# Moving the operands of a feed-forward block to other SBUF addresses: two pads, a pool for the statistics, two small buffers fewer

## The chip, the cores and the metric

The kernel runs on one core of a Trainium2 chip. The metric is the device time of one execution in microseconds; the number to compare is the median of several runs. Five engines take part: TensorE (PE in the profile; PEld is its loading of weights), VectorE (DVE), ScalarE (ACT), GpSimd (POOL) and SyncE (SP), which issues most of the DMAs. SBUF is the on-chip memory that PE, DVE, ACT, POOL and the DMAs share; a tile in it occupies the same byte range in each of 128 partitions, so that one number, its start within the partition, gives its address.

## What is computed

One transformer block over x of shape (4, 1024, 256), in float32: attention with 16 heads, then a gated feed-forward part with ternary weights and two square hidden layers of 1024 x 1024. Cut to what matters:

```python
x = x + layernorm(attention(layernorm(x), Wqkv, Wout))
# feed-forward part, on y = layernorm(x); tlin(x, w, s) = einsum('bsi,oi->bso', x, w) * s
h = silu(tlin(y, w1_w, w1_s)) * tlin(y, w2_w, w2_s)      # 256 -> 1024
h = gelu(tlin(h, h1_w, h1_s))                            # 1024 -> 1024
h = gelu(tlin(h, h2_w, h2_s))                            # 1024 -> 1024
x = x + layernorm(tlin(h, w3_w, w3_s))                   # 1024 -> 256
```

## The kernel before

Everything is unrolled; the order of instructions on each engine is the order in which the Python code issues them, and semaphores are placed where one engine's result is another's input. `tile_fast` does the whole block. `tile_general` is a fallback that runs only when a flag computed on the chip is set; in the traced execution it isn't.

**Attention** takes the four batches in turn, to about 575 us. For each batch and group of four heads, line 536 makes the scores `s` from the stacked tiles `sq` and `sk`, line 537 exponentiates them into a ring of eight half-tiles `e`, and line 544 weighs the values, `acc <- e, vaug`. Preparing the next batch (line 321 projects `xT` with `wqk_sb` and `wv_sb`), rounding the feed-forward weights and dividing by the sums (`quotients`, with its small tile `den`) are put between as side steps.

**The feed-forward part** then takes each batch of 1,024 tokens as two halves of 512. Its matmuls run on float32r values: each float32 operand is split into a rounded part `hi` (line 936, ScalarE) and a remainder `lo` (line 940, VectorE), and both are multiplied with the same ternary weights, which are exact.

- `gated`: line 966 multiplies `x_in` (four tiles that were `cq`/`ck` in the attention) with `w1` and `w2` (also in former `cq`/`ck` tiles) into the PSUM tile `pg`; ScalarE's silu and one VectorE instruction follow. Per batch 128 matmuls of 128x128 weights against 128x512 columns.
- `Layer.run`, twice: the square layers are done with a scheme of seven block products in place of eight. The weights' seven factors were made during the attention, lie in DRAM, and come by DMA (`load_factor`) into a ring of four slots, which are the former `sq`/`sk` tiles (`ring_of`). Line 1045 multiplies them with the `hi` and `lo` of sums of hidden blocks, into the PSUM tile `ph`. Per batch 448 matmuls of the same form as those of `pg`. The weights are the stationary operand and are loaded for each matmul; the `hi` or `lo` block is the moving operand, whose columns are streamed.
- `finish`: line 1153 multiplies the last hidden blocks (here the stationary operand) with `w3_sb` (the moving one, 256 columns) into `pz`, 128 matmuls per batch; layer norm, residual and store follow.

The hidden blocks (`Half`: `g`, `hi`, `lo`, `t2`, `c`, `u`, `w`, each [128, 2, 512] of 4 bytes, 4,096 bytes per partition) come from a free list of 22 places. Eight, `a0` to `a7`, are opened on the left side of SBUF where the ring `e` was, fourteen, `b0` to `b13`, by `open_ffn` in the pool `fb` on the right side, where the attention's pools `aw` and `work` were. Pools are laid one behind another, from the left upwards and from the right downwards, and each tile takes the next multiple of 32 bytes. So the small tiles ahead of a large one decide its address modulo 256:

| tiles | start modulo 256, before | after |
|---|---|---|
| `cq`/`ck` (in `gated`: x_in, w1, w2), `sq`/`sk` (ring of factors), ring `e`, `a0` to `a7` | 128 | 0 |
| `w3_sb` | 32 | 0 |
| `b` blocks | 160 (one), 32 (three), 224 (ten) | 0 |
| `xT`, `xn`, `top`, `wr`, `vaug`, `on`, `wqk_sb`, `wv_sb`, `wo_sb`, `cv`, `folded`, `oT` | 160 | 0 |
| `x0` to `x3` (inputs and residuals) | 224 | 224 |

Each operand's start within such a tile is a multiple of 512 bytes further on in lines 966, 1045 and 1153, so it has the tile's remainder.

`Norms` holds the small statistics of the layer norms (`mv`, `st`, `ve`, `rstd`, `nb`); its attribute `small` says which pool they come from. In the feed-forward part that is `fb`, where they lie between the `b` blocks, six buffers each.

Of the kernel before, what the change touches and what calls it, by code (L numbers as in the profile page):

```python
# [10 lines left out]
F32 = mybir.dt.float32  # L11
# [8 lines left out]
P = 128  # L20
HEADS = 16
DH = 16
SLOT = 32
# [14 lines left out]
NQ = 512  # L38
# [5 lines left out]
@with_exitstack  # L44
def tile_attention_ffn_block(ctx: ExitStack, tc: tile.TileContext, x, wqk, wv, wo, w1, w1s, w2, w2s, h1, h1s, h2, h2s, w3, w3s, out):

    nc = tc.nc
    B, S, D = x.shape
    bad = ctx.enter_context(tc.tile_pool(name="flag", bufs=1)).tile([1, 1], I32, name="bad")
    tile_fast(tc, x, wqk, wv, wo, w1, w1s, w2, w2s, h1, h1s, h2, h2s, w3, w3s, out, bad)
    failed = nc.values_load(bad[0:1, 0:1], min_val=0, max_val=1 << 24)
    with tc.If(failed > 0):  # L70
        tile_general(tc, x, wqk, wv, wo, w1, w1s, w2, w2s, h1, h1s, h2, h2s, w3, w3s, out)
# [58 lines left out]
def tile_fast(ctx: ExitStack, tc: tile.TileContext, x, wqk, wv, wo, w1, w1s, w2, w2s, h1, h1s, h2, h2s, w3, w3s, out, bad):  # L130
# [12 lines left out]
    small = ctx.enter_context(tc.tile_pool(name="small", bufs=3))  # L143
# [28 lines left out]
    norms = Norms(nc, const, small)  # L172
# [23 lines left out]
    with ExitStack() as actx, ExitStack() as rctx:  # L196
        aw = actx.enter_context(tc.tile_pool(name="aw", bufs=1, side="right"))
# [50 lines left out]
        on = [aw.tile([P, DC, NQ // SLOT, SLOT], F32, name=f"on{h}") for h in range(NH)]  # L248

        heads_bf = aw.tile([P, SLOT], BF16, name="heads_bf")  # L250
        nc.vector.memset(heads_bf, 0.0)
        own = small.tile([P, HPT], F32, tag="own", name="own", bufs=1)
        nc.vector.tensor_reduce(own, ident.rearrange("p (h d) -> p h d", d=DH), AX.X, ALU.add)
# [304 lines left out]
        def quotients(g, h, em, o):  # L558

            o = o.rearrange("p (j s) -> p j s", s=SLOT)  # L560
            den = small.tile([P, NQ // SLOT], F32, tag="den", name="den")
            n = P // SLOT
            nc.vector.scalar_tensor_tensor(den[:, 0:n], em, SM_EPS, o[:, 0:n, DH], ALU.mult, ALU.add)
            nc.vector.tensor_copy(den[:, n:], o[:, n:, DH])
            nc.vector.reciprocal(den, den)
            e = DH * (g % GPT)
            nc.vector.tensor_mul(on[h][:, g // GPT, :, e : e + DH], o[:, :, 0:DH], den.unsqueeze(2).to_broadcast([P, NQ // SLOT, DH]))
# [3 lines left out]
        def divide(g, h, o, top):  # L571


            there = shuffle.tile([HPG, P, P], F32, tag="top", name="top_d")
            folded = work.tile([P, P // SLOT, P], F32, tag="folded", name="folded", bufs=1)
            nc.sync.dma_start(out=there.rearrange("i k q -> k i q"), in_=top.rearrange("p u n q -> p (u n) q"))

            mine = divided["made"]
            divided["made"] += 1

            def back():
                nc.sync.dma_start(out=folded, in_=there.rearrange("i (k s) q -> (i k) s q", s=P // SLOT))

            def fold():
                for n in (2, 1):
                    nc.vector.tensor_max(folded[:, 0:n], folded[:, 0:n], folded[:, n : 2 * n])
                nc.vector.transpose(folded[:, 1], folded[:, 0])

            def run():
                em = small.tile([P, P // SLOT], F32, tag="em", name="em")  # L590
                nc.vector.tensor_reduce(em, folded[:, 1].rearrange("p (j k) -> p j k", k=SLOT), AX.X, ALU.max)
                quotients(g, h, em, o)
                divided["done"] += 1

            begun = Step(back, 2, False)
            begun.ready = lambda: divided["done"] == mine
            return [begun, Step(fold, 2, False, work=1.2), Step(run, 1, False, work=1.4)]

        def divide_last(g, h, o, top):


            def run():
                turned = work.tile([P, P // SLOT, P], F32, tag="folded", name="turned", bufs=1)
                flat, n = top.rearrange("p u n q -> p (u n q)"), HPG * P // SLOT
                nc.vector.transpose(turned.rearrange("p s q -> p (s q)"), flat)
                nc.vector.tensor_reduce(flat[:, 0:n], turned.rearrange("p s (j k) -> p (s j) k", k=SLOT), AX.X, ALU.max)
                parts = flat[0:SLOT, n : n + n * P // SLOT].rearrange("p (k n) -> p k n", n=n)
                for k in range(P // SLOT):
                    nc.vector.tensor_copy(parts[:, k], flat[SLOT * k : SLOT * (k + 1), 0:n])
                most = flat[0:SLOT, P : P + n]  # L610
                nc.vector.tensor_reduce(most, parts.rearrange("p k n -> p n k"), AX.X, ALU.max)
                most = most.rearrange("p (i j) -> p i j", i=HPG)
                em = small.tile([P, P // SLOT], F32, tag="em", name="em")
                for i in range(HPG):
                    nc.vector.tensor_copy(em[SLOT * i : SLOT * (i + 1), :], most[:, i])
                quotients(g, h, em, o)

            return [Step(run, 1, False)]

        def ending(b, h, copy):  # L620
# [61 lines left out]
            if b < B - 1:  # L682

                return steps + [Step(lambda: side.add(tail), 0, False)]
            opened = Step(open_ffn, 0, False)
            opened.ready = lambda: not ends[b, 0][0]
            return steps + ([opened] if h == NH - 1 else []) + tail
# [65 lines left out]
        side = Side()  # L753
# [94 lines left out]
        def load_weights(n, chunks=None):  # L848
            for c in range(len(homes[n])) if chunks is None else chunks:
                nc.sync.dma_start(out=homes[n][c].bitcast(F32), in_=rounded[n][c * P : (c + 1) * P, :].bitcast(F32))  # L850
# [10 lines left out]
        def open_ffn():  # L861

            actx.close()
            fb = ctx.enter_context(tc.tile_pool(name="fb", bufs=1, side="right", reuse_waits="tile"))
            free.extend((fb, f"b{i}") for i in range(14))
            w3_sb = fb.tile([P, HC, D], F32R, name="w3_sb")
            homes["w3"] = [w3_sb[:, c, :] for c in range(HC)]
            load_weights("w3")
            ffn["fb"] = fb
            norms.small, norms.bufs = fb, 6  # L870

        def norm_steps(tiles, st):

# [794 lines left out]
```

## Time and profile before

| what | value |
|---|---|
| median of 3 runs (lowest, highest) | 1205.7 us (1205.09, 1208.14) |
| the profiled execution: its own time, its span | 1206.14 us, 1204.4 us |
| mean granted TensorE clock | 0.994 |
| busy: PE, PEld, DVE, ACT, POOL | 1160.6, 709.1, 845.9, 886.2, 298.7 us |
| DMA moved | 163.66 MB, mean 136 GB/s |
| chain that ended last, largest parts | PE 71%; by line: PE ph L1045 35%, PE acc L544 10%, PE pg L966 9% |

The span is the time from the first to the last instruction of the profiled execution; its own time adds what lies around it. The duration given for a matmul includes the time until its result has drained: a matmul of `ph` has a duration of 394 ns in the middle, while the next one starts long before that. What a matmul costs when they follow each other closely is therefore the distance from its start to the next one's, which the timeline's first column and the chain of waits give. In the chain, a row is a run of instructions of one group, with its start, its length and its count.

### The profile page before, as it was taken

What the parts mean: (1) busy time and instruction counts of PE and PEld (TensorE: products, weight loads), DVE (VectorE), ACT (ScalarE), POOL (GpSimd) and SP (SyncE); (2) the same over time, 40 slices, a digit from 0 to 9 for tenths busy, and PEclk for the clock granted to TensorE, in tenths of its full rate; (3) what the DMA queues carried; (4) which work ended last, traced back from release to release, by engine and by line L of the source; (5) the groups of instructions that cost most, each with busy time, mean ns of one, the idle gap of its engine ahead of it and who ended that gap; (6) DMA issues with size and microseconds to landing.
All of it is one profiled execution on the core that took longest, in us unless ns stands there. A gap on an engine that the chain in (4) does not pass through costs nothing.

```text
span 1204.4 us, 21320 instructions
## 1 busy us (share of the span) xinstructions
PE 1160.6 (96%) x7994; PEld 709.1 (59%) x7994; DVE 845.9 (70%) x1501; ACT 886.2 (74%) x1050; POOL 298.7 (25%) x458
## 2 busy tenths in 40 slices
PE   8999999999999999998999999999999999999994
PEld 3333333333333333332678889888898888988884
DVE  4577777785878867767585756867678676785765
ACT  4999888988999989998466575576756767567660
POOL 6454256565566643220000000000000000000000
PEclk9999999999999999999999999999999999999997
DMA  5877655676666664472314441354522545225401
GB/s 144 214 185 185 150 134 157 163 178 163 155 175 164 167 166 105 106 176 88 105 36 140 134 147 57 101 175 153 179 74 85 177 154 176 74 84 187 157 24 38
DMA packets 78672, 163.66 MB, mean 136 GB/s; under 512 B 14688, under 2 KB 40928, under 8 KB 78560
## 3 DMA queue, kind: packets, MB, share of 16 engines
q1 hardware_dynamic: 62832, 120.18, 34.9%
q0 software_dynamic: 15200, 41.50, 12.6%
q8 instruction: 65, 1.06, 0.4%
q10 hardware_dynamic: 528, 0.52, 0.1%
q14 instruction: 47, 0.39, 0.1%
HBM read 98.71 MB, written 29.88 MB: 107 GB/s over the span
## 4 chain that ended last, share of the span: by engine, by line
PE 71%; DVE 10%; ACT 9%; issue 4%; DMA 3%; SPq 2%; POOL 1%; ACTq 0%; POOLq 0%; DVEq 0%
PE ph L1045 35%; PE acc L544 10%; PE pg L966 9%; ACT e L537 8%; PE s L536 7%; PE pz L1153 4%; PE p L321 2%; DVE top L556 2%; PE py L321 2%; SPq L482 1%; PE pv L321 1%; DVE st L97 1%; DMA x<-in_x_dram 1%; DMA sq<-cq0hi 1%; PE fpt L909 1%
## 5 line engine op out<-in xcount | busy, mean ns | idle before, releaser
L537 ACT ACTIVATE e<-s 128x1024 f32<-128x1024 f32 x512 | 483.0, 1046 | 43.8 <-PE s L536 34.1
L544 PE MATMUL acc<-e,vaug 128*32 128x512 f32 (+1 forms) x2424 | 256.6, 535 | 1.4 <-DVE o L798 1.4
L107 POOL TENSOR_TENSOR rstd<-ve,minus_half 128x4 f32<-128x4 f32 (+1 forms) x34 | 38.3, 1126 | 700.6 <-DVE ve L105 596.2
L536 PE MATMUL s<-sq,sk 64*128 64x512 f32 x1024 | 188.9, 445 | 20.7 <-ACT e L537 19.5
L536 PEld LDWEIGHTS s<-sq,sk 64*128 64x128 f32 x1024 | 87.3, 184 | 167.9 <-ACT e L537 147.4
L1045 PE MATMUL ph<-hi,sq 128*128 128x512 f32 x448 | 177.8, 397 | 0.0
L1045 PE MATMUL ph<-lo,sq 128*128 128x512 f32 x448 | 176.7, 394 | 0.0
L1045 PE MATMUL ph<-hi,sk 128*128 128x512 f32 x448 | 176.6, 394 | 0.0
L1045 PE MATMUL ph<-lo,sk 128*128 128x512 f32 x448 | 176.5, 394 | 0.0
L556 DVE TENSOR_TENSOR top<-top,e 128x512 f32<-128x512 f32 x192 | 140.1, 730 | 21.1 <-ACT e L537 15.4
L544 PEld LDWEIGHTS acc<-e,vaug 128*32 128x32 f32 x2424 | 61.9, 109 | 117.4 <-issue 107.4
L940 DVE TENSOR_TENSOR lo<-g,hi 128x1024 fp32r<-128x1024 f32 x48 | 58.8, 1224 | 57.8 <-ACT hi L936 57.8
L1045 PEld LDWEIGHTS ph<-lo,sk 128*128 128x128 f32 x448 | 84.1, 188 | 20.0
L1045 PEld LDWEIGHTS ph<-hi,sk 128*128 128x128 f32 x448 | 84.1, 188 | 20.0
L1045 PEld LDWEIGHTS ph<-hi,sq 128*128 128x128 f32 x448 | 84.1, 188 | 19.5
L1045 PEld LDWEIGHTS ph<-lo,sq 128*128 128x128 f32 x448 | 84.2, 188 | 19.2
L1033 ACT ACTIVATE c<-ph,h_scale 128x512 f32<-128x512 f32 x64 | 40.5, 684 | 55.8 <-PE ph L1045 55.8
L940 DVE TENSOR_TENSOR lo<-c,hi 128x1024 fp32r<-128x1024 f32 x48 | 58.2, 1219 | 25.8 <-ACT hi L936 25.8
L968 ACT ACTIVATE sg<-pg,w_scale 128x512 f32<-128x512 f32 x64 | 43.9, 687 | 41.6 <-PE pg L966 38.2
L321 PE MATMUL p<-xT,wqk_sb 128*32 128x512 f32 x512 | 65.7, 593 | 0.5 <-ACT xT L324 0.5
L969 DVE SCALAR_TENSOR_TENSOR g<-pg,w_scale,sg 128x512 f32<-128x512 f32 x64 | 47.7, 747 | 22.1 <-ACT sg L968 22.1
L1153 PE MATMUL pz<-w_sb,hi 128*128 128x256 f32 x256 | 60.1, 279 | 0.0
(189 smaller groups left out, 1830.0 us busy)
## 6 DMA issues: line engine op xcount, KB each, us to landing
sq<-h_f SPq DMA_DIRECT2D x56, 512.0 KB, 3.9
sk<-h_f SPq DMA_DIRECT2D x56, 512.0 KB, 4.7
w<-in_h_dram POOLq DMA_DIRECT2D x32, 256.0 KB, 4.9
h_f<-wr POOLq DMA_DIRECT2D x16, 512.0 KB, 3.7
x<-in_h_dram SPq DMA_DIRECT2D x16, 512.0 KB, 3.6
top_d<-top SPq DMA_DIRECT2D x30, 256.0 KB, 2.5
folded<-top_d SPq DMA_DIRECT2D x30, 256.0 KB, 3.6
h_f<-wr POOLq DMA_DIRECT2D x16, 384.0 KB, 3.8
```

The lines of the kernel that those rows point to most:

```text
L321: nc.tensor.matmul(o[j : j + SLOT, :], w[:, j : j + SLOT], i, **flags)
L536: nc.tensor.matmul(s[:, a, :], stacks[1, g % 2, u][r, c * P : (c + 1) * P], stacks[0, g % 2, u][r, h * NQ : (h + 1) * NQ], start=True, sto ...
L537: nc.scalar.activation(pair(k)[:, u], s, AF.Exp)
L544: nc.tensor.matmul(acc[SLOT * i : SLOT * (i + 1), q0:q1], vaug[g % 2][:, c, i, :], pair(k)[:, i // 2, i % 2, q0:q1], start=c == 0 and q0 = ...
L556: nc.vector.tensor_max(top, top if c > 1 else pair(k - 2)[:, :, :, 0:P], pair(k)[:, :, :, 0:P])
L940: nc.vector.tensor_sub(self.lo[i].t, self.raw[i].t, self.hi[i].t.bitcast(F32))
L966: nc.tensor.matmul(p[:, k, :], homes[n][d][:, m * P : (m + 1) * P], half[:, d, :], start=d == j == 0, stop=d == DC - 1 and j == 1)
L968: nc.scalar.activation(sg, p[:, 0, :], AF.Silu, scale=scales["w1"][:, m : m + 1])
L969: nc.vector.scalar_tensor_tensor(x[i, h][c // 2].t[:, c % 2, :], p[:, 1, :], scales["w2"][:, m : m + 1], sg, ALU.mult, ALU.mult)
L1033: nc.scalar.activation(o.t[:, j, :], (o.t if src is None else src)[:, j, :], AF.Gelu, scale=scale[:, m : m + 1])
L1045: nc.tensor.matmul(p[:, j, :], w, half, start=start and c == n == 0, stop=c == HC // 2 - 1 and n == 1, skip_group_check=True,)
L1153: nc.tensor.matmul(p[:, j, :D], half[:, (t0 + j) * P : (t0 + j + 1) * P], homes["w3"][c], start=c == order[0] and n == 0, stop=c == order[ ...
```

## The change

It adds a tile of 160 bytes per partition at the end of the pool `aw` and one of 32 bytes at the beginning of a new pool `fs`; neither is used. `fs` is opened by `open_ffn` ahead of `fb` and takes the statistics of the feed-forward part, which no longer lie between the `b` blocks. `den` has one buffer in place of three (64 bytes each), so that everything behind it on the left side starts 128 bytes earlier. The starts that result are in the table above.

```diff
@@ -248,6 +248,7 @@
         heads_bf = aw.tile([P, SLOT], BF16, name="heads_bf")
+        aw.tile([P, 40], F32, name="even")
         nc.vector.memset(heads_bf, 0.0)
@@ -558,7 +559,7 @@
-            den = small.tile([P, NQ // SLOT], F32, tag="den", name="den")
+            den = small.tile([P, NQ // SLOT], F32, tag="den", name="den", bufs=1)
@@ -861,13 +862,15 @@
             actx.close()
+            fs = ctx.enter_context(tc.tile_pool(name="fs", bufs=1, side="right", reuse_waits="tile"))
+            fs.tile([P, 8], F32, name="even")
             fb = ctx.enter_context(tc.tile_pool(name="fb", bufs=1, side="right", reuse_waits="tile"))
             free.extend((fb, f"b{i}") for i in range(14))
             w3_sb = fb.tile([P, HC, D], F32R, name="w3_sb")
             homes["w3"] = [w3_sb[:, c, :] for c in range(HC)]
             load_weights("w3")
             ffn["fb"] = fb
-            norms.small, norms.bufs = fb, 6
+            norms.small, norms.bufs = fs, 6
```

## The prediction

> **What bounds the kernel now.** I read the engine shares first, then the chain that ended last in order of time, then a table of engine busy time by stretch, then TensorE's rows in order of time. TensorE (PE) is busy 1160.6 us of 1204.4, 96%. The first half (to about 575 us) is attention, in which ScalarE's exponentials run almost as full as PE. In the feed-forward half PE stands alone: in the stretch from 585 to 1182 us it is busy 595.27 of 597.00 us, beside 417.10 for VectorE, 374.70 for ScalarE and a DMA share of 0.36. From 617.95 us on the chain is nothing but matmuls:
>
> ```profile
> 724.08 14.85 PE pz L1153 x128
> 738.93 29.06 PE pg L966 x128
> 768.00 33.49 PE ph L1045 x144
> ...
> 806.29 48.32 PE ph L1045 x208
> ...
> 1068.73 89.15 PE ph L1045 x384
> ```
>
> The columns are start, length, engine, output tile, line, count. Dividing length by count gives the time from one matmul's start to the next: pg 29.06/128 = 227.0 ns; ph 33.49/144 = 232.6, 48.32/208 = 232.3, 89.15/384 = 232.2 ns; pz (256 columns, not 512) 14.85/128 = 116.0 ns. pg and ph have the same form, 128x128 weights against 128x512 float32r columns, yet ph is 5 ns dearer. In this half any nanosecond off a matmul comes off the end, so the question is what these 5 ns are.
>
> Here the profile has to be read with the table of addresses above. Line 1045 has 1,792 matmuls in the trace and 1,792 in the program, so the n-th of one is the n-th of the other, and every row gets its operands' addresses. All of pg's operands, weights and columns, lie at 128 mod 256. ph's weights do too, but its columns lie in blocks at 128, 160, 32 or 224. Here is ph with all four of its column blocks at 224, and then with all four at 128:
>
> ```profile
> 700.67 0.39 PE L1045 MATMUL ph<-hi,sq 128*128 128x512 f32 x1
> 700.90 0.39 PE L1045 MATMUL ph<-lo,sq 128*128 128x512 f32 x1
> ...
> 703.94 0.40 PE L1045 MATMUL ph<-hi,sk 128*128 128x512 f32 x1
> 704.17 0.39 PE L1045 MATMUL ph<-lo,sk 128*128 128x512 f32 x1
> ```
>
> ```profile
> 718.48 0.39 PE L1045 MATMUL ph<-hi,sk 128*128 128x512 f32 x1
> 718.71 0.39 PE L1045 MATMUL ph<-lo,sk 128*128 128x512 f32 x1
> ...
> 722.11 0.39 PE L1045 MATMUL ph<-hi,sk 128*128 128x512 f32 x1
> 722.33 0.39 PE L1045 MATMUL ph<-lo,sk 128*128 128x512 f32 x1
> ```
>
> Sixteen matmuls of the first are 15 steps in 3.50 us, 233.3 ns each; eighteen of the second are 17 steps in 3.85 us, 226.5 ns each. Over all of ph (steps of up to 260 ns) the mean by the column block's place is 231.1 ns at 128 (612 steps), 233.2 at 160 (80), 234.5 at 32 (256), 233.7 at 224 (837). All 20 blocks sort this way: the eight at 128 lie between 229.6 and 232.6, the twelve others between 232.6 and 235.3.
>
> The blocks at 128 are not at 226.7 in the mean because a block at another place leaves something behind. A stretch of operands that all lie at 128, entered after one that does not, steps 233, 236, 224, 231, 236, 228, 233, 231 ns (231.5 in the mean) and then falls to 226-227 and stays. The longest such stretch has 33 matmuls: seven longer steps, then 226 or 227 to its end. I counted pairs of successive steps within such stretches: from 226-227 none of 47 left it in ph and 2 of 407 in pg; of the others 4 of 132 in ph and 11 of 64 in pg fell into it. So the cheap rhythm holds while operands lie alike, and ph is mixed all the time.
>
> **The change part by part.**
>
> **Instructions.** Engine by engine, the changed program has the same instructions in the same order with the same waits in everything that the trace shows executed; only waits ahead of the fallback, which doesn't run, are arranged otherwise. Hence the single buffer for `den` costs nothing: its four users are all VectorE instructions, in order, and no wait comes in. The two pads are never read or written. The statistics in `fs` are small tiles used by VectorE, GpSimd and ScalarE, and no wait comes in for them either. What is left is addresses: every operand of ph, pg and pz goes to 0 mod 256.
>
> **ph.** 1,772 steps of up to 260 ns have a mean of 232.3 ns (411.6 us); 20 longer ones wait for data or follow a pause, and I leave them. No row of the trace has an operand at 0 mod 256. The nearest is 128, the only other place that is a multiple of 64, with pg as a whole stage in which all operands lie alike: 227.3 ns (497 steps). I take that: 1,772 x 5.0 ns = **8.8 us**.
>
> **pz.** 511 steps, mean 116.9 ns. Its moving operand w3_sb (at 32) meets weights at 224, 128, 32 and 160. In the first batch, with weights at 224 only, sixteen in a row step 113-114 ns, half of 226.7; with weights at 128 or 32 it is 116 to 121. At 113.5 the gain is 511 x 3.4 ns = **1.7 us**.
>
> **pg.** Already 227.3; I take nothing (226.7 would be 0.3 us).
>
> **Attention.** Its fp32 matmuls (acc, p, pv, py) have a step of 429-430 ns for four of 512 columns whether the columns lie at 128 (e) or 160 (xT): place doesn't show there, nothing taken. The float32r scores s have all operands at 128 already and step 231 or 235-236 ns behind the fp32 ones; 328 steps of that kind at 6 ns could give 2.0 us, but PE waits 19.5 us for the exponentials there, so part is hidden. I take 0, and 2 us either way for the range.
>
> **Other engines.** VectorE's lo takes 1218 to 1227 ns for every mix of places, ScalarE's hi 1043 to 1051, the gelu 684 at all four: nothing to gain, and nothing that PE would then wait for, since 10 us less PE time raises VectorE's share of this stretch from 417/597 to 417/587 only. The factor loads (512 KB, 3.9 to 4.7 us from issue to landing) have four ring slots ahead of products of 7.4 us.
>
> **Sum.** 8.8 + 1.7 = 10.5 us, all on the chain. The profiled execution took 1206.14 us, of which 1204.4 is span and 1.7 lies around it; the median 1205.7 is 0.4 below it. 1205.7 - 10.5 = **1195.2 us**.
>
> **Two rules weighed.** The row: 226.5 ns where all lies at 128, 233.3 where columns lie at 224. The Trainium skill's page "SBUF — State Buffer" says under "Who interferes with whom" that "PE and ACT never wait on anyone", and under "Operand start alignment" it asks only for a multiple of the element size and calls that legality, not speed. By these rules address is nothing and the sum is 0: 1205.7 us. The row contradicts them in this trace, so I go by the row, and keep the rule as a rival. Second, "TensorE: Matmul & The Clock Gate", in "Wait — 56ns, not 53.3ns?", puts a warm matmul's step at columns / 2.4 GHz plus about 2.5 ns, 215.7 ns for 512 columns. The fp32 rows agree if 512 fp32 columns are counted as 1,024 (429-430 ns), the best float32r row doesn't (226.7, which is 215.7 plus 11). If that rest came from 128 not being a multiple of 256, ph would give 1,772 x 16.6 = 29.4 us, pg 497 x 11.6 = 5.8, pz 511 x 7.7 = 3.9, in all 39 us: 1166.6 us, an estimate by that page. Since 226.7 is seen at a steady 544 cycles of 2.4 GHz, 17 for every 16 columns, it looks like the form's own rate rather than a fault of place. It is the lower end, unlikely.
>
> **Rivals.**
> **Half a gain.** Places no longer disturb, but the dearer rhythm is kept alive by other things (the pauses of about 90 ns between products, ScalarE and VectorE in the same memory). Then ph stays at what its stretches of equal places have now, 230.0 ns: 1,772 x 2.3 = 4.1, and pz gives about 0.8: 1200.8 us. For it: stretches at 128 begin with the longer steps. Against: pg has such pauses too and stays at 227.3.
> **No change.** Either the rule holds and order, not place, makes the difference, or 0 mod 256 keeps the dearer rhythm everywhere: 231.5 ns for ph and pg, 118 for pz gives 1.4 - 2.1 - 0.6 = -1.3 us, 1207.0. Against: twenty blocks sorted by place.
> **Slower: weights and columns meet.** Weights and columns are read at the same time (PEld is busy while PE is), and now both start at 0 mod 256 everywhere. If equal places made them collide, as pz's 118 to 121 ns with weights and w3_sb both at 32 may show, steps would go to the worst seen in bulk, 236 and 120.5: 6.6 + 4.3 + 1.8 = 12.7 us more, 1218.4. It decides from a mean step of 231.5 ns over all three on (584.5 us over 2,525 steps of 512 columns), and from 232.9 it is measurably slower. Against: pg has both at 128 and runs cheapest of all.
>
> **How the numbers follow.** Full gain (1193 to 1198): 0.63. Half a gain (1198 to 1203): 0.14. No change: 0.11. Slower: 0.06. A gain beyond 226.7: 0.06. The range 1190 to 1202.5 holds the first, nearly all of the second and the nearer part of the last, eight in ten. A measurement of this kernel tells from no change about 0.3%, 3.6 us: faster 0.82 (full, beyond, most of half), within it 0.12, slower 0.06.
>
> **What would show it.** Right: ph's groups on the chain at 227 to 228 ns by length over count, pz at 113 to 114, pg still 227, all earlier times on the chain up to 575 us within 2 us. Half: ph at 230. Wrong in size: any step near 216, or pg moved. Wrong altogether: ph at 232 with its columns at 0, or gaps in PE where it now ran through (waits on hi or lo).

## The result and the profile after

The changed kernel takes 1199.88 us (median of 6 runs, 1197.99 to 1202.45), the kernel before 1207.06 us (6 runs, 1205.09 to 1210.02): a ratio of 0.9935, 95% interval 0.9923 to 0.9947. The change is faster by about 7.8 us; 10.5 were predicted.

The same stages of the feed-forward part in the chain of waits of the changed kernel (start, length, engine, output, line, count; line 966 is now 969, 1045 is 1048, 1153 is 1156):

```profile
722.61 15.35 PE pz L1156 x128
737.96 29.04 PE pg L969 x128
767.00 32.66 PE ph L1048 x144
...
1063.82 87.04 PE ph L1048 x384
```

Length over count gives what a matmul costs: ph 32.66/144 = 226.8 and 87.04/384 = 226.7 ns, where it was 232.6 and 232.2; pg 226.9, where it was 227.0; pz 15.35/128 = 119.9 ns, where it was 116.0. So the square layers gained what they could, and the last layer lost. In the timeline of the changed kernel the last layer's starts stand 0.12 us apart:

```profile
729.76 0.28 PE L1156 MATMUL pz<-w_sb,lo 128*128 128x256 f32 x1
729.88 0.28 PE L1156 MATMUL pz<-w_sb,hi 128*128 128x256 f32 x1
...
731.08 0.28 PE L1156 MATMUL pz<-w_sb,hi 128*128 128x256 f32 x1
731.20 0.28 PE L1156 MATMUL pz<-w_sb,lo 128*128 128x256 f32 x1
```

Twelve steps in 1.44 us are 120.0 ns each. Over all matmuls, leaving out steps of more than 260 ns (the granted clock is 1.00 from 618 to 1178 us in every run of this document, so it is no cause of what differs here):

| | ph, 1,772 steps | pg, 497 steps | pz, 511 steps |
|---|---|---|---|
| before | 232.29 ns, 411.6 us | 227.34 ns, 113.0 us | 116.95 ns, 59.8 us |
| after | 227.00 ns, 402.2 us | 227.25 ns, 112.9 us | 119.94 ns, 61.3 us |

That is -9.4 us for ph and +1.5 us for pz, -7.9 in sum. The span fell by 7.2 us only (1204.4 to 1197.2), because the attention half of this execution ended 0.6 us later: the first ph of the chain starts at 618.54 us instead of 617.95. From there to the end it is 578.7 instead of 586.4 us, 7.7 less. PE stays the bound. Of its waits in the feed-forward part (the view of waits, PE alone, 585 to 1182 us: who waits for whom, us in total, times, longest) the only row is, as before the change (there with a longest wait of 1.0),

```profile
PE pg L969 <- DVE g L972: 1.7, 2, 0.9
```

The attention half starts the feed-forward part anywhere between 617 and 622 us in the runs below, with the kernel's own scatter. I therefore compare the **feed-forward stretch**, the time from the first ph row of the chain to the span's end. One kernel profiled twice (`w3_32` and the timed version below) had 577.4 and 577.2 us of it.

### The profile page after: what moved, and what is told of

It is laid out like the page before. It is cut to its first block, busy times and chain, and to the rows that moved or that the text cites. A ratio compares the mean times of both kernels' runs of the same rounds, so it can differ in the third digit from the quotient of the medians.

```text
span 1197.2 us, 21320 instructions
## 1 busy us (share of the span) xinstructions
PE 1153.3 (96%) x7994; PEld 710.4 (59%) x7994; DVE 842.7 (70%) x1501; ACT 886.4 (74%) x1050; POOL 297.8 (25%) x458
## 4 chain that ended last, share of the span: by engine, by line
PE 68%; ACT 9%; DVE 7%; DMA 6%; issue 4%; POOL 4%; SPq 1%; ACTq 0%; POOLq 0%; DVEq 0%
PE ph L1048 34%; PE acc L545 9%; PE pg L969 9%; ACT e L538 8%; PE s L537 6%; PE pz L1156 4%; PE p L322 2%; PE py L322 2%; DMA h_f<-wr 1%; DMA w<-in_h_dram 1%; PE pv L322 1%; DVE top L557 1%; DMA x<-in_x_dram 1%; SPq L483 1%; DMA sk<-ck0lo 1%
## 5 line engine op out<-in xcount | busy, mean ns | idle before, releaser
L943 DVE TENSOR_TENSOR lo<-g,hi 128x1024 fp32r<-128x1024 f32 x48 | 58.8, 1224 | 54.6 <-ACT hi L939 54.6
L943 DVE TENSOR_TENSOR lo<-c,hi 128x1024 fp32r<-128x1024 f32 x48 | 58.2, 1219 | 24.2 <-ACT hi L939 24.2
L1156 PE MATMUL pz<-w_sb,lo 128*128 128x256 f32 x256 | 61.6, 283 | 0.0
```

The lines of the kernel that those rows point to most:

```text
L943: nc.vector.tensor_sub(self.lo[i].t, self.raw[i].t, self.hi[i].t.bitcast(F32))
L1156: nc.tensor.matmul(p[:, j, :D], half[:, (t0 + j) * P : (t0 + j + 1) * P], homes["w3"][c], start=c == order[0] and n == 0, stop=c == order[ ...
```

## The experiments

The theory at the start was the prediction's: the cheap rhythm, 226.7 ns, needs columns at multiples of 64. All runs but the last are a single execution each, so what is read from them is the steps. Each diff below is against the changed kernel. The kernel before, run on the same chip beside them, took 1210.2 us (beside `left_only`, `all128`, `all32`, `w3_64`), 1206.4 (beside `c32_w0`, `c128_w0`, `w3_128`, `w3_192`) and 1209.88 (beside `w3_32`, `w3_160`, `w3_224`).

**One part alone (`left_only`).** Only `den` keeps one buffer; the pad in `aw`, the pool `fs` and its pad are gone. The left side moves to 0, the `b` blocks stay at 160, 32 and 224.

```diff
-        aw.tile([P, 40], F32, name="even")
-            fs = ctx.enter_context(tc.tile_pool(name="fs", bufs=1, side="right", reuse_waits="tile"))
-            fs.tile([P, 8], F32, name="even")
-            norms.small, norms.bufs = fs, 6
+            norms.small, norms.bufs = fb, 6
```

> One part alone: one buffer for den, so cq/ck, the ring of factors and the a blocks lie at 0; the b blocks stay at 160, 32 and 224, w3_sb at 32, and no pool fs. Theory (the cheap rhythm needs the columns of successive matmuls to lie at multiples of 64): pg 227.3 ns a step, ph still 232 (mixed), pz 116 to 118; time 1206 to 1208 us. Rival (0 for the weights is what counts): ph near 227, time near 1197.

1208.62 us. Its chain:

```profile
727.02 15.06 PE pz L1153 x128
742.09 29.05 PE pg L966 x128
771.14 33.36 PE ph L1045 x144
...
1071.28 89.05 PE ph L1045 x384
```

ph is at 231.7 and 231.9 ns (mean 231.78), pz at 117.3: nearly as before the change (232.29 and 116.95). Moving the weights and eight of the 22 blocks to 0 does next to nothing while the other fourteen lie elsewhere.

**Another common place (`all128`).** The left side at 128 as before the change, and the right side moved to 128 too. Against the kernel before, this adds only the pool `fs` with its pad.

```diff
-        aw.tile([P, 40], F32, name="even")
-            den = small.tile([P, NQ // SLOT], F32, tag="den", name="den", bufs=1)
+            den = small.tile([P, NQ // SLOT], F32, tag="den", name="den")
-            fs.tile([P, 8], F32, name="even")
+            fs.tile([P, 40], F32, name="even")
```

> All operands of pg, ph and pz at 128 mod 256, the places of the left side as before the change, the b blocks and w3_sb moved to 128. Theory (128 is as good as 0 for 512 columns): ph and pg 227.0, pz 120 as after the change, time 1199 to 1201 us. Rival (256 is needed): ph 230 or more, time 1205.

1199.32 us, ph 226.95, pg 227.35, pz 119.94 ns, stretch 578.7 us, all as in the changed kernel. Two rows of its chain:

```profile
722.89 15.35 PE pz L1155 x128
...
1064.06 87.04 PE ph L1047 x384
```

So the gain is in putting the `b` blocks where the rest is, and multiples of 256 are not what counts.

**A common place that is no multiple of 64 (`all32`).** A pad of 32 bytes ahead of `cq`, and everything on the right at 32.

```diff
+        keep.tile([P, 8], F32, name="shift")
-        aw.tile([P, 40], F32, name="even")
-            fs.tile([P, 8], F32, name="even")
+            fs.tile([P, 64], F32, name="even")
```

> All operands of pg, ph and pz at 32 mod 256, alike but at no multiple of 64. Theory (a multiple of 64 is needed): ph and pg 231 to 234, time 1207 to 1212 us. Rival (it is enough that operands lie alike): ph and pg 227, time 1200.

1201.34 us. The theory fell, the rival stands:

```profile
725.02 15.35 PE pz L1156 x128
740.37 29.04 PE pg L969 x128
769.41 32.66 PE ph L1048 x144
...
1066.18 87.04 PE ph L1048 x384
```

Each of these rows has the changed kernel's length to the hundredth of a microsecond. At 32 mod 256 the matmuls are as cheap as at 0 or 128, provided that all operands are there; the stretch is 578.6 us. So none of the three places is bad in itself. Two readings are left: (A) the columns of successive matmuls must lie alike, or (B) columns must lie where the weights lie.

**Columns alike, but not where the weights are (`c32_w0`, `c128_w0`).** Two runs keep the weights and all of pg at 0, and put all 22 blocks at 32 or at 128. `w3_sb` is put where it tells something about pz besides.

```diff
-        aw.tile([P, 40], F32, name="even")
-            fs.tile([P, 8], F32, name="even")
+            fs.tile([P, 64], F32, name="even")        # 40 for columns at 128
             w3_sb = fb.tile([P, HC, D], F32R, name="w3_sb")
+            fb.tile([P, 40], F32, name="shift_w3")    # 56
+        fa.tile([P, 8], F32, name="shift_a")          # 32
         free.extend((fa, f"a{i}") for i in range(8))
```

> ph's columns all at 32, its weights at 0; pg all at 0; w3_sb 96 above pz's weights (128 against 32). Theory A (it is enough that the columns of successive matmuls lie alike): ph 227, time near 1199 us. Theory B (columns must lie where the weights lie, their distance decides): ph 229 to 234 ns, 402 us of ph become 406 to 415, time 1204 to 1212. pz as a function of the distance of w3_sb above the weights: if 0 is the worst place (120.0), 96 gives 113.3 to 119.

> ph's columns all at 128, its weights at 0; pg all at 0; w3_sb 32 above pz's weights (160 against 128). Theory A (columns alike is enough): ph 227. Theory B (distance to the weights decides, modulo 256): ph not at 227; if modulo 64 or 128, ph 227. Time 1199 or 1204 to 1212 us. pz at a distance of 32: 113.3 to 120.

1213.52 us at 32 and 1208.9 us at 128. The chain with columns at 32:

```profile
744.12 29.05 PE pg L969 x128
773.18 33.60 PE ph L1048 x144
...
1075.39 89.60 PE ph L1048 x384
```

and with columns at 128:

```profile
740.59 29.02 PE pg L969 x128
769.61 33.60 PE ph L1048 x144
...
1070.90 89.60 PE ph L1048 x384
```

ph is at 233.3 ns in both (means 233.29 and 233.06), dearer than in the mixed kernel before, while pg, with its weights and columns at 0, stays at 227. (A) is out: the columns are all alike. Nor is it the columns' own place: at 32 they cost 226.94 ns in `all32`, at 128 they cost 226.95 in `all128`, and only the weights lie elsewhere here. (B) holds for the three distances that a whole run kept in ph: 0, 32 and 128. The period of the distance isn't 128, because columns at 128 and weights at 0 are about as dear as a distance of 32. It needn't be more than 256: by the program's addresses ph's columns in the changed kernel lie 0 or 256 above the weights modulo 512, and step 226.99 ns (609 steps) and 227.00 (1,163). The starts in the timeline of `c128_w0` show the dear rhythm:

```profile
630.99 0.40 PE L1048 MATMUL ph<-lo,sq 128*128 128x512 f32 x1
631.23 0.40 PE L1048 MATMUL ph<-hi,sq 128*128 128x512 f32 x1
631.46 0.39 PE L1048 MATMUL ph<-lo,sq 128*128 128x512 f32 x1
...
632.62 0.40 PE L1048 MATMUL ph<-hi,sk 128*128 128x512 f32 x1
632.86 0.40 PE L1048 MATMUL ph<-lo,sk 128*128 128x512 f32 x1
```

Eight steps in 1.87 us, 233.8 ns. Single steps repeat a pattern of seven here to within 1 ns, 229, 230, 232, 241, 233, 231, 231; further on about 229 and 238 alternate. So regular a pattern is no noise, and the view of waits shows none of PE's for another engine from 620 us on in this run.

**The last layer.** pz has 256 columns to each load of weights, and 119.94 ns at a common place. Six runs leave everything else at 0 and move `w3_sb` alone, by an unused tile behind it:

```diff
             w3_sb = fb.tile([P, HC, D], F32R, name="w3_sb")
+            fb.tile([P, 48], F32, name="shift_w3")    # 48: w3_sb at 64; 56: 32; 32: 128; 24: 160; 16: 192; 8: 224
```

> As after the change, with 192 unused bytes behind w3_sb, so that w3_sb lies at 64 and everything else at 0. In the kernel before, pz stepped 113.3 ns where its weights lay 64 below w3_sb modulo 256 (224 against 32). Theory (weights and columns at one place collide in the short matmuls): pz 113.3 to 114 instead of 120, 511 x 6.3 ns = 3.2 us off, time 1196.7 us. Rival (pz's step follows the place of the weights alone): pz stays at 120, time 1199.9.

> As after the change, w3_sb at 128, pz's weights at 0. ph and pg 227. If pz's step follows the distance of w3_sb above its weights, and in the kernel before 118 was seen at a distance of 128 (32 against 160), pz is 118; if the distance counts modulo 128 only, 120 as at 0. Time 1199 to 1201 us.

> As after the change, w3_sb at 192, pz's weights at 0. ph and pg 227. pz: by distance nothing like it was seen in the kernel before; if the distance counts modulo 128, 117.8 as at 64; if a distance exists at which a load of weights misses all reads of columns, 113.3 and 3.4 us less, 1196.5 us. Else 1199 to 1201.

> As after the change, w3_sb at 32, pz's weights at 0 (distance 32). ph and pg 227. Theory B (the distance of the columns above the weights, modulo 256, decides, not the places themselves): pz in the cycle 113, 116, 118, 120 of c128_w0, which had the same distance at other places, mean 116.7, 1.7 us less than at distance 0. Rival (the places themselves matter too): another mean than 116.7.

> As after the change, w3_sb at 160, distance 160. ph and pg 227. In the kernel before, pz had about 118 at this distance (32 against 128). Theory B: 117 to 119, time within 1 us of w3_64's 1200.5 or w3_192's 1196.7 as the day's scatter allows.

> As after the change, w3_sb at 224, distance 224, which no run has had in pz. ph and pg 227. If short and long matmuls shared a rule, a distance of 224 (-32) would be about as good as 32, 116.7; no theory of mine gives a number, bounds 113.3 and 122.

ph stayed at 226.94 to 227.02 ns in all six. pz, by how far `w3_sb` lies above the weights modulo 256:

| distance | pz step, ns | run, its time, us | feed-forward stretch, us |
|---|---|---|---|
| 0 | 119.94 | the change, 1199.88 (6 runs) | 578.7 |
| 32 | 116.69 | w3_32, 1198.53 | 577.4 |
| 64 | 117.80 | w3_64, 1200.54 | 578.0 |
| 128 | 119.95 | w3_128, 1197.82 | 578.8 |
| 160 | 118.70 | w3_160, 1199.68 | 578.1 |
| 192 | 117.77 | w3_192, 1196.73 | 577.7 |
| 224 | 118.32 | w3_224, 1199.90 | 578.2 |

The single times scatter by more than what is sought (w3_192 is the lowest because its attention half ended at 617.23 us); the steps and the stretch tell it. A distance of 32 gave 116.69 ns here with weights at 0 and `w3_sb` at 32, and the same 116.69 with 128 and 160 in `c128_w0`; a distance of 0 gave 119.94 at each of the three common places. So where one distance holds throughout, the mean followed the distance and not the places. The pattern of single steps didn't: 116, 117, 117 here, 113, 116, 118, 120 there. A distance of 96 (weights at 32, `w3_sb` at 128, in `c32_w0`) gave 120.04. Distances that are 128 apart agree at 0 and 128 and at 64 and 192, but not at 32 and 160 or 96 and 224, so 128 is no period here either. Of what was forecast, the mean of w3_32 (116.7) and the range of w3_160 came; the 118 for w3_128 and the 116.7 for w3_224 didn't.

The theory ahead of w3_64 fell, and so did its rival: neither 113.3 nor 120 came, but 117.80. In the kernel before, a distance of 64 (weights at 224, `w3_sb` at 32) had given two values. In the first batch fifteen steps take 1.70 us, 113.3 ns each:

```profile
724.86 0.28 PE L1153 MATMUL pz<-w_sb,hi 128*128 128x256 f32 x1
...
726.56 0.28 PE L1153 MATMUL pz<-w_sb,lo 128*128 128x256 f32 x1
```

In the third, 23 steps take 2.71 us, 117.8 ns each, which is what w3_64 has:

```profile
1031.07 0.28 PE L1153 MATMUL pz<-w_sb,hi 128*128 128x256 f32 x1
...
1033.78 0.28 PE L1153 MATMUL pz<-w_sb,lo 128*128 128x256 f32 x1
```

More than one rhythm can hold at one distance; what chooses between them isn't shown.

**The version that follows from it,** with `w3_sb` at 32 and the rest at 0 (`w3_32_timed`), was run six times.

> The kernel with the cheapest steps seen in ph, pg and pz together (w3_sb at 32, everything else at 0), timed. By the steps: ph 402.1 us (before 411.6), pg 113.0 (113.0), pz 59.6 (59.8), in all 9.7 us less than before and 1.7 less than the change alone: ratio to before 0.992, 1198 us where before takes 1207. Rival (the gain of pz is lost behind it): ratio 0.9935 as the change alone.

1198.33 us (6 runs, 1197.18 to 1199.99) beside 1207.62 (11 runs): a ratio of 0.9925, interval 0.9912 to 0.9938. Its chain:

```profile
722.16 14.93 PE pz L1157 x128
737.09 29.04 PE pg L970 x128
766.13 32.64 PE ph L1049 x144
...
1062.06 87.04 PE ph L1049 x384
```

pz is down from 15.35 to 14.93 us for 128 matmuls, four times over, 1.7 us; the rest is as after the change. The stretch, 577.2 us, is 1.4 below the changed kernel's (taken before rounding). The two ratios' intervals overlap, so the timing alone doesn't separate the two; the steps do.

## Why the prediction was right in direction and too large

- **What bounds it, and that everything saved on PE comes off the end:** right. The sum over ph and pz, -7.9 us, is close to the fall of the feed-forward stretch, -7.7, and of the median, -7.2 (-7.8 by the ratio).
- **Instructions at nothing** (`den`, the pads, the statistics' pool): right. PE got no new wait in the feed-forward part, and pg kept its time.
- **ph, 8.8 us at 227.3 ns:** right in the term, 9.4 us at 227.0: 1,651 of 1,772 steps are now 226 or 227 ns, where it was 105. The means by place that stand behind it (231.1, 233.2, 234.5, 233.7) count 1,785 steps, not 1,772: thirteen pauses of 313 to 320 ns are in them. Without these they are 230.7 at 128, 232.1 at 160, 233.3 at 32 and 233.2 at 224; 128 stays the cheapest.
- **pz, 1.7 us at 113.5 ns:** wrong, and it is the term that makes the sum too large: it cost 1.5 us instead, 119.94 ns. I took one stretch of sixteen matmuls, with weights at 224 and `w3_sb` at 32, as the value for operands that lie alike. They didn't lie alike there: they were 64 apart. And the same pair of places stood at 117.8 ns in the third batch, which I passed over instead of asking why.
- **The reason, "a multiple of 64":** wrong. The run with everything at 32 has ph at 226.94 ns. I had compared columns by their own place because the weights were at 128 throughout ph, where place and distance from the weights say the same thing. That ph's term came out is in part luck: the change happens to satisfy both readings. By a multiple of 64 alone `c128_w0` would have been as cheap, and it has 233.06 ns. The sentence that the cheap rhythm holds while operands lie alike was the right one for ph, and it means weights and columns.
- **The rival "weights and columns meet":** it was given 0.06 with a loss of 12.7 us. Its price came true in pz, 119.94 ns against the 120.5 assumed. Its mechanism isn't shown by that, because pz costs the same at distances of 96 and 128, where the operands don't start at one place. In ph the common place is the cheapest of those tried. I had treated one rule as valid for 512 and for 256 columns.
- **"Half a gain"** is where the time lies (1198 to 1203 us), but not its cause: it would have shown ph at 230 ns, and ph is at 227.0. A full gain in ph and a loss in pz gave that time. A rate beyond 226.7 is out too: no step mean of ph in any run is below 226.94.
- **The rule that PE never waits on anyone** (the Trainium skill, "SBUF — State Buffer", "Who interferes with whom") speaks of engines that hold each other up, which no run here tests. That address is therefore nothing doesn't follow: in ph the same instructions cost 226.95 ns (`all128`) or 233.29 (`c32_w0`) by nothing but the addresses of PE's own two operands.
- **Other engines, taken at nothing:** right. The groups of VectorE's lo have means of 1219 to 1224 ns before and after.
- **Attention, taken at nothing:** it ended 0.6 us later in the profiled execution, within the 617 to 622 us over which all runs scatter. The traces show no effect of the move on its matmuls. The prediction's 429-430 ns for four fp32 matmuls is one of two values: of the groups of four acc matmuls of 512 columns that another acc group follows, 180 took about 430 ns and 117 about 454. After the change it is 180 and 119, though their distances went from 96 and 224 to 0 and 128. The starts of successive scores s lie 144.1 ns apart in the mean before and 144.3 after.

What stays open is the mechanism. In the profile each load of ph's weights (188 ns in the middle) runs beside a matmul, and the dependence of the step on the distance between weights and columns is shown. That the two collide in the memory is an inference that no run tests; why 256 columns have another order of distances than 512 isn't shown either, nor what ph does at distances other than 0, 32 and 128.

## What to carry to other kernels

Before moving an operand for the sake of alignment, compare the places of the operands that are read together: here moving weights and columns to one place modulo 256 was worth 9.4 us in matmuls of 512 float32r columns, and 0, 32 and 128 did equally well. The best distance belongs to one shape: the same move cost 1.5 us in matmuls of 256 columns. So each shape's step has to be read from the trace (start to start, by address), and its operands moved by themselves. And where a trace shows two values for one pair of addresses, the lower one is no forecast.

## What the runs showed that I had not expected

- Alignment beyond a multiple of 32 bytes was worth nothing in itself: three common places, 0, 32 and 128, agree within 0.06 ns a step in ph and within 0.1 us over the feed-forward stretch of 578.7 us.
- With columns uniformly away from the weights, the cost of a matmul repeats in a short pattern over long stretches, and its mean at distances of 32 and 128 (233.29 and 233.06 ns) is above that of the mixture before the change (232.29).
- No run held pz at 113.3 ns a step: of the eight distances kept throughout, the best is 32, with 116.69.
